# Softmax division of a two-layer graph-attention kernel: all batches on ScalarE, one planner entry per head, and a planner with durations read from a trace

## The chip, the cores and the metric

The kernel runs on one core of one Trainium2 chip. A core has five engines that work side by side and wait for each other through semaphores: TensorE (PE, matmul; its weight loads are shown as PEld), VectorE (DVE), ScalarE (ACT), GpSimd (POOL) and SyncE (SP, which here issues nearly all DMA transfers). The metric is the device time of one execution in microseconds (us). The kernel before takes 2100.86 us, the median of three runs (2097.80 to 2101.08).

## The reference

The input x is 128 batches of a 128 x 512 matrix in fp32, adj is one 128 x 128 adjacency matrix. Layer 0 is a graph step with a maximum, and a layer norm. Layer 1 is masked multi-head attention with a projection, two residual sums and two layer norms:

```python
# layer 0: A = adj @ x[b], C = A + bias
x = layernorm(x + max_over_columns(relu(A[:, None, :] + (C - A)[:, :, None])))
# layer 1: 8 heads of 64 columns
q, k, v = split(x @ w_qkv)
attn = softmax(where(adj == 0, -inf, q @ k.T * 64 ** -0.5))
o = (attn @ v) @ w_proj + b_proj
x = layernorm(x + o + layernorm(o) * gamma + beta)
```

The part that changes is the softmax: of each row of 128 scores in each of 8 heads, the exponentials are divided by their sum.

## The kernel before

**Groups.** The 128 batches are worked in 32 groups of 4. A group is the unit of the main loop (lines 1205 to 1256), and the loop is software-pipelined. One turn p holds, in TensorE's order: the attention product with v of group p-1 (`attend`), the scores of group p (`scores`), v of group p (`v_unit`, seven products instead of eight, with sums of inputs made on GpSimd) with layer 0's matmuls of group p+2 (`l0_mm`) in between, the projection of group p-1 (`o_unit`, also seven products), and q and k of group p+1 (`qk_unit`, 26 products instead of 32; `NODES` and `EDGES` say which product is added to which PSUM bank).

**Names.** k0 to k7 are the eight PSUM banks. u0 to u5 are SBUF copies of banks ("snapshots", ScalarE). s0 to s3 hold the softmax of the four batches of a group. x0 and x1 hold two batches each of layer 0's input, loaded from DRAM in `load`. hl0 to hl8 and so0, so1 are the sums that feed the matmuls. z, xr0 and xr1 belong to the last layer norm (`tails`).

**Softmax, lines 990 to 1076.** For each batch VectorE scales the scores and adds the mask (two instructions on two banks, line 996), then takes the row maximum of all heads (line 1015). ScalarE makes the exponential of each head with its sum (eight instructions, line 1024). VectorE inverts the sums (line 1034). The division follows as eight instructions on 128 x 128 elements: for batches 0 and 2 of a group on ScalarE (`activation` with Identity and a scale column, line 1041), for batches 1 and 3 on VectorE (`tensor_scalar`, line 1043). The table `DIV` (line 988) says which. Then VectorE transposes 32 x 32 blocks into pu (line 1053), SP stores pu to DRAM (hop) and loads it back in four pieces in transposed place into the same s slot, which `attend` of the next turn reads.

**Layer 0 for a later group.** x0 and x1 are read by `l0_mm` and by the layer-norm statistics (`bn`, VectorE, line 430), normalised in place (ScalarE, line 472), transposed in blocks into xt (VectorE, line 507), stored to xhop and loaded back as x1T in four pieces each (SP); then GpSimd adds beta in place and SP spills them to DRAM (`l0_beta_spill`). Only then may SP load the next input into the slot.

**What sets the order.** All work is first recorded with `plan.add(engine, cost, emit, reads, writes)`. Predecessors come from the logs of the buffers. `Plan.run` gives every entry a due time (from the end backwards, with TensorE's entries in a fixed order) and then list-schedules: at each step the engine that can start first takes, of its ready entries, the one due first. Costs, a lag per engine (`LAG`), and for DMAs a shared wire of 270 KB per us (lines 199 and 239 to 241) are its clock. Entries are emitted in that order and each engine keeps it: an engine waits at its next instruction, whatever is ready behind it. One planner entry may be several instructions. Before the change the exponentials and the divisions are entries of four instructions each (lines 1021 to 1047).

**A reuse that the planner does not see.** In `qk_unit` the snapshot of node 1 takes slot u4 (line 751). In the turn's record it comes before `o.closing()`, which is called after node 2 (`between`, line 1252) and whose VectorE result (line 867) still reads the o unit's own snapshot in slot u4 (first the end of `qk_unit`'s loop over the nodes, then the main loop). On the chip the snapshot of node 1 waits for that result.

```python
for fn in between.get(n, ()):
    fn()
...
between = {2: [o.closing]}
```

Of the kernel before, what the change touches and what calls it, by code (L numbers as in the profile page):

```python
# [133 lines left out]
class Op:  # L134
    __slots__ = ("eng", "cost", "lat", "emit", "preds", "succs", "n", "due", "start", "done", "size")

    def __init__(self, n, eng, cost, emit, size):
        self.n, self.eng, self.cost, self.emit, self.size = n, eng, cost, emit, size
        self.preds, self.succs = set(), []
        self.due = self.start = self.done = None  # L140
# [17 lines left out]
class Plan:  # L158
# [5 lines left out]
    def add(self, eng, cost, emit, reads=(), writes=(), size=0):  # L164
        op = Op(len(self.ops), eng, cost, emit, size)
        for accesses, writing in ((reads, False), (writes, True)):
            for a in accesses:
                buf, key = a if type(a) is tuple else (a, None)
                for other, k, w in buf.log:
                    if (w or writing) and (k is None or key is None or k == key):  # L170
                        op.preds.add(other)
                if buf.before is not None and (writing or not buf.log):
                    op.preds.update(o for o, _, _ in buf.before.log)
                buf.log.append((op, key, writing))
        if eng == "PE":
            if self.pe is not None:
                op.preds.add(self.pe)
            self.pe = op
        op.preds.discard(op)
        self.ops.append(op)  # L180
        return op

    LAG = {"PE": 0.27, "DVE": 0.2, "ACT": 0.2, "POOL": 0.15, "SP": 2.2}
    RATE = 0.27

    def run(self, lead):
# [11 lines left out]
        for op in reversed(ops):  # L198
            lag = self.LAG[op.eng] + (op.size / 270.0 if op.size else 0.0)
            due = min((s.due - (0.02 if s.eng == op.eng == "PE" else lag) for s in op.succs), default=end)  # L200
            if op in ideal:
                due = min(due, ideal[op] + op.cost)
            op.due = due - op.cost
        free = dict.fromkeys(self.LAG, 0.0)
        wire = 0.0
# [13 lines left out]
        while todo:  # L219
# [18 lines left out]
            seen = op.done + self.LAG[e]  # L238
            if op.size:
                wire = max(wire, op.done) + op.size / 270.0  # L240
                seen = wire + 2.2
# [12 lines left out]
def kernel(  # L254
# [62 lines left out]
    def dma(dst, src, reads=(), writes=(), kb=512, queue=None, cost=0.47):  # L317
        eng, q = ("ACT", A) if queue == "ACT" else ("SP", SY)
        return plan.add(
            eng, cost, lambda: pin(q.dma_start(out=dst(), in_=src())), reads, writes, size=kb  # L320
        )
# [15 lines left out]
    dma(lambda: adj_sb.t, lambda: adj, [], [adj_sb], 64)  # L337
# [5 lines left out]
    def load(q, queue=None, split=False):  # L343
        b = xs[q] = buf(X_SLOT.get(q, f"x{q % 2}"), [P, 2, D])
        if split:
            for j in range(2):
                dma(lambda j=j: b.t[:, j], lambda j=j: x[2 * q + j], [], [(b, j)], 256, queue)
        else:
            dma(
                lambda: b.t,  # L350
                lambda: x[ds(2 * q, 2)].rearrange("j p d -> p j d"),
                [],
                [(b, 0), (b, 1)],
            )

    load(0, "ACT", True)
    dma(lambda: bias0.t, lambda: l0_b.unsqueeze(1), [], [bias0], 1)
    load(1, None, True)

    def broadcast(name, src, queue=None):  # L360
        b = buf(name, [P, D])
        dma(lambda: b.t, lambda: src.partition_broadcast(P), [], [b], 256, queue)
# [45 lines left out]
    def l0_mm(f, k):  # L408
# [10 lines left out]
        plan.add("DVE", 0.64, lambda: pin(V.tensor_reduce(am.t, b.t, AX.X, ALU.max)), [b], [am])  # L419
# [8 lines left out]
    def bn(src, reads, mv, c):  # L428
        st = small("st", 6)
        plan.add("DVE", 0.64, lambda: pin(V.bn_stats(st.t, src())), reads, [st])  # L430
        plan.add("DVE", 0.17, lambda: pin(V.bn_aggr(mv.t[:, c], st.t)), [st], [(mv, c)])  # L431
# [66 lines left out]
    def l0_transpose(q):  # L498
# [3 lines left out]
        for j in range(2):  # L502
            plan.add(
                "DVE",
                0.64,
# [10 lines left out]
        for i in range(Q):  # L516
# [5 lines left out]
                128,  # L522
            )
        xT = x1T_buf(g)
        for i in range(Q):
# [5 lines left out]
                128,  # L531
# [4 lines left out]
    def l0_transpose_pe(f, k):  # L536
# [5 lines left out]
        def emit():  # L542
# [7 lines left out]
            0.64,  # L550
# [9 lines left out]
    def l0_beta_spill(q):  # L560
# [3 lines left out]
            2.45,  # L564
# [5 lines left out]
        dma(lambda: s.t, lambda: xb.t, [xb], [s])  # L570
# [11 lines left out]
    def weight_forms():  # L582
# [14 lines left out]
        def add(dst, dst_at, a, b, sa, sb_):  # L597
# [3 lines left out]
            if sa < 0 and sb_ < 0:  # L601
                plan.add(
                    "DVE",
                    0.66,
# [9 lines left out]
            if turn % 5 < 3:  # L614
                plan.add("DVE", 0.66, lambda: tt(V, dst(), pa(), pb(), op), reads, [dst_at])
            else:
                plan.add("POOL", 0.74, lambda: tt(GP, dst(), pa(), pb(), op), reads, [dst_at])
# [38 lines left out]
    def qk_plain(h, banks, eng):  # L656

        xT = x1T_buf(0)
        for n in range(4):
# [19 lines left out]
            else:  # L679
                plan.add(  # L680
                    "DVE", 0.64, lambda b=b, n=n: pin(V.tensor_copy(dst.t[:, n], halves(b))), [b], [(dst, n)]
# [4 lines left out]
    def token_sums(g):  # L686
# [6 lines left out]
        for n, (a, b, s) in enumerate(SUMS):  # L693
# [4 lines left out]
                0.74,  # L698
# [15 lines left out]
    def qk_unit(g, phys, between=()):  # L714
# [4 lines left out]
        for n, (prods, lb, chain, seeds, adds, block_) in enumerate(NODES):  # L719
# [14 lines left out]
            if block_ is None:  # L734
                for y, s in mine:
# [3 lines left out]
                        0.66,  # L739
# [16 lines left out]
            else:  # L756
# [3 lines left out]
                for y, s in sorted(mine):  # L760
                    u = snaps[y][0]
                    s = s * SIGN[n]
                    if first:
                        plan.add(
                            "DVE",
                            0.66,
# [12 lines left out]
                    else:  # L779
                        plan.add(  # L780
                            "POOL",
                            1.28,
# [18 lines left out]
    def weight_load(w, src, col):  # L801
        rows = src.rearrange("(d c p) e -> d p c e", d=2, p=P)
        for i, d, c in ((0, 0, 0), (3, 0, HE), (1, 1, 0), (2, 1, HE)):
# [5 lines left out]
                256,  # L809
# [12 lines left out]
    class Unit:  # L822
# [40 lines left out]
        def result(self, half, col):  # L863
# [5 lines left out]
                0.64,  # L869
# [27 lines left out]
    def v_unit(g, phys):  # L897
# [7 lines left out]
        for dst, p, q_, op in (  # L905
# [7 lines left out]
                1.28,  # L913
# [14 lines left out]
    def o_unit(g, phys):  # L928
# [6 lines left out]
        for dst, p, q_, op in (  # L935
# [7 lines left out]
                1.28,  # L943
# [44 lines left out]
    DIV = {0: "ACT", 1: "DVE", 2: "ACT", 3: "DVE"}  # L988

    def softmax(b, bs):  # L990
        s = buf(f"s{b % 4}", [P, 2, NP, P])
        for par in range(2):
            plan.add(
                "DVE",
                0.64,
# [9 lines left out]
                [(s, par)],  # L1005
# [3 lines left out]
        def flat():  # L1009
# [4 lines left out]
            1.17,  # L1014
# [4 lines left out]
        for par in range(2):  # L1019

            def emit(par=par):
                for i in range(4 * par, 4 * par + 4):
                    pin(
                        A.activation(  # L1024
                            flat()[:, i],
                            flat()[:, i],
                            AF.Exp,
                            bias=nm.t[:, i : i + 1],
                            accum_out=sm.t[:, i : i + 1],
                        )  # L1030
                    )

            plan.add("ACT", 1.55, emit, [nm, (s, par)], [(s, par), (sm, par)])
        plan.add("DVE", 0.17, lambda: pin(V.reciprocal(rec.t, sm.t)), [sm], [rec])
        for par in range(2):

            def emit(par=par, eng=DIV[b % 4]):
                for i in range(4 * par, 4 * par + 4):
                    p, r = flat()[:, i], rec.t[:, i : i + 1]
                    if eng == "ACT":  # L1040
                        pin(A.activation(p, p, AF.Identity, scale=r))
                    else:
                        pin(V.tensor_scalar(p, p, r, None, ALU.mult))  # L1043

            plan.add(
                DIV[b % 4], 1.15 if DIV[b % 4] == "ACT" else 0.72, emit, [rec, (s, par)], [(s, par)]
# [4 lines left out]
            1.22,  # L1051
# [14 lines left out]
            [hop],  # L1066
        )
        t = pT[b] = buf(f"s{b % 4}", [P, Q, H, QS])
        for q in range(Q):
# [5 lines left out]
                128,  # L1075
# [30 lines left out]
    def reload(q, slot):  # L1106
        r, s = buf(slot, [P, 2, D]), spilled.pop(q)
        dma(lambda: r.t, lambda: s.t, [s], [r])
        return r

    def tails(g):
# [7 lines left out]
        for h in range(2):  # L1119
# [5 lines left out]
            for j in range(2):  # L1125
# [9 lines left out]
                2.45,  # L1135
# [4 lines left out]
            plan.add("POOL", 2.45, lambda z=z, o=o: tt(GP, z.t, z.t, o.t, ALU.add), [z, o], [z])  # L1140
            plan.add("POOL", 2.45, lambda z=z, r=r: tt(GP, r.t, r.t, z.t, ALU.add), [z, r], [r])
# [140 lines left out]
    dma(wl, lambda: w_proj.rearrange("(c p) e -> p c e", p=P), [], [(lastw, "w")], 1024)  # L1282
# [3 lines left out]
    for q in range(2 * g - 2, 2 * g + 2):  # L1286
# [4 lines left out]
        dma(ap, lambda s=s: s.t, [s], [(lastw, q)], 512)  # L1291
# [8 lines left out]
    def tail_pool(b, o, j):  # L1300
# [6 lines left out]
        for with_, op, rd in (  # L1307
# [5 lines left out]
                "POOL", 1.28, lambda with_=with_, op=op: tt(GP, z(), z(), with_(), op), [zk, rd], [zk]  # L1313
# [3 lines left out]
    def outer(b, zk, z, mz):  # L1317
# [3 lines left out]
        dma(lambda: out[b], z, [zk], [], 256)  # L1321
# [114 lines left out]
```

## Time and profile before

| | |
|---|---|
| median of three runs | 2100.86 us |
| the profiled execution | 2098.84 us |
| its span, first to last instruction | 2097.0 us |
| mean granted TensorE clock | 0.975 |
| busy: PE, PEld | 1932.3 us (92%), 1614.5 us (77%) |
| busy: DVE, ACT, POOL | 1523.7 us (73%), 1339.5 us (64%), 1568.2 us (75%) |
| division on ScalarE, line 1041 | 512 instructions, 159.4 us |
| division on VectorE, line 1043 | 512 instructions, 226.8 us |
| exponentials, line 1024 | 1024 instructions, 395.7 us |
| DMA | 341.87 MB, mean 163 GB/s |

Busy time adds the durations of an engine's instructions; overlapping ones are counted once. In the timeline a row is one instruction or a run of equal ones: start and length in us, engine, source line, operation, output<-inputs with buffer numbers left out, count, and in brackets how long the engine was idle before it and what ended that. Most work that goes through a helper has the helper's line (309, 312, 315, 320), so the tile names tell instructions apart. SPq rows are DMA issues, not transfers. Times inside a turn are given below relative to the first attention matmul of that turn, which is at 1000.54 us in the turn that is used as the example.

### The profile page before, as it was taken

What the parts mean: (1) busy time and instruction counts of PE and PEld (TensorE: products, weight loads), DVE (VectorE), ACT (ScalarE), POOL (GpSimd) and SP (SyncE); (2) the same over time, 40 slices, a digit from 0 to 9 for tenths busy, and PEclk for the clock granted to TensorE, in tenths of its full rate; (3) what the DMA queues carried; (4) which work ended last, traced back from release to release, by engine and by line L of the source; (5) the groups of instructions that cost most, each with busy time, mean ns of one, the idle gap of its engine ahead of it and who ended that gap; (6) DMA issues with size and microseconds to landing.
All of it is one profiled execution on the core that took longest, in us unless ns stands there. A gap on an engine that the chain in (4) does not pass through costs nothing.

```text
span 2097.0 us, 35142 instructions
## 1 busy us (share of the span) xinstructions
PE 1932.3 (92%) x11307; PEld 1614.5 (77%) x11307; DVE 1523.7 (73%) x2906; ACT 1339.5 (64%) x3893; POOL 1568.2 (75%) x1634
## 2 busy tenths in 40 slices
PE   9989899999999989999999999999999999999995
PEld 7777787777787777877778778778777787787883
DVE  8677666777676876767776677766687776777664
ACT  2666565766666666667666667666667665676764
POOL 8657776787776877777777778777777787687856
PEclk9999999999999999999999999999999999999998
DMA  7763466644567445675455764446654456744553
GB/s 220 199 161 106 133 165 201 176 141 147 142 199 201 132 143 149 181 201 169 136 139 161 201 194 137 146 147 181 201 162 142 141 160 201 195 135 131 145 172 128
DMA packets 444855, 341.87 MB, mean 163 GB/s; under 512 B 276736, under 2 KB 378240, under 8 KB 444672
## 3 DMA queue, kind: packets, MB, share of 16 engines
q1 hardware_dynamic: 444384, 339.11, 56.1%
q8 instruction: 90, 1.47, 0.3%
q14 instruction: 93, 0.76, 0.1%
q10 hardware_dynamic: 288, 0.52, 0.1%
HBM read 172.82 MB, written 166.72 MB: 162 GB/s over the span
## 4 chain that ended last, share of the span: by engine, by line
PE 60%; DVE 26%; ACT 5%; DMA 3%; issue 3%; POOL 2%; SPq 1%; ACTq 0%; DVEq 0%; POOLq 0%
PE k L315 60%; DVE s L1043 7%; DVE nm L1015 5%; DVE am L419 3%; DMA x<-in_x_dram 3%; DVE st L430 2%; DVE pu L1053 2%; DVE v L309 2%; SPq L320 1%; ACT s L1024 1%; ACT z L472 1%; DVE qk L312 1%; ACT u L752 1%; POOL x L309 1%; ACT k L748 1%
## 5 line engine op out<-in xcount | busy, mean ns | idle before, releaser
L315 PE MATMUL k<-hl,wqk 128*128 128x256 f32 x2232 | 520.2, 382 | 1.4 <-ACT k L748 1.4
L315 PEld LDWEIGHTS k<-hl,wqk 128*128 128x128 f32 x2232 | 423.6, 191 | 67.7 <-issue 9.4
L1024 ACT ACTIVATE s<-s,nm 128x128 f32<-128x128 f32 x1024 | 395.7, 390 | 3.5 <-DVE nm L1015 3.2
L315 PE MATMUL k<-wv,hl 128*128 128x256 f32 x1024 | 268.8, 410 | 78.9 <-DVE v L309 75.3
L752 ACT COPY u<-k 128x512 f32<-128x512 f32 x341 | 190.1, 589 | 215.6 <-DVE qk L312 142.9
L315 PEld LDWEIGHTS k<-wv,hl 128*128 128x128 f32 x1024 | 204.8, 203 | 146.8 <-DVE v L309 87.3
L315 PE MATMUL k<-x1T,wqk 128*128 128x256 f32 x992 | 252.5, 388 | 58.9 <-ACT u L752 57.8
L309 POOL TENSOR_TENSOR z<-z,ga_bc 128x1024 f32<-128x1024 f32 x60 | 142.0, 2366 | 200.5 <-ACT z L472 200.5
L312 DVE SCALAR_TENSOR_TENSOR qk<-k,u 128x512 f32<-128x512 f32 x248 | 168.4, 687 | 157.4 <-ACT u L752 87.1
L315 PEld LDWEIGHTS k<-x1T,wqk 128*128 128x128 f32 x992 | 187.6, 193 | 99.0 <-ACT u L752 70.3
L315 PE MATMUL k<-wp,so 128*128 128x256 f32 x992 | 241.4, 393 | 0.1
L312 DVE SCALAR_TENSOR_TENSOR s<-k,mask 128x512 f32<-128x512 f32 x256 | 156.4, 682 | 115.3 <-PE k L315 115.1
L309 POOL TENSOR_TENSOR hl<-x1T 128x512 f32<-128x512 f32 (+1 forms) x250 | 216.9, 874 | 28.1 <-PE k L315 16.9
L1043 DVE TENSOR_SCALAR s<-s,rec 128x128 f32<-128x128 f32 x512 | 226.8, 512 | 1.2
L315 PEld LDWEIGHTS k<-wp,so 128*128 128x128 f32 x992 | 199.7, 202 | 32.5 <-DVE o L309 0.8
L309 POOL TENSOR_TENSOR x<-x,be_bc 128x1024 f32<-128x1024 f32 x62 | 146.5, 2362 | 89.4 <-DVE mvo L431 76.7
L309 POOL TENSOR_TENSOR hl<-x1T,hl 128x512 f32<-128x512 f32 (+1 forms) x249 | 196.8, 801 | 0.0
L1024 ACT ACTIVATION_READ_ACCUMULATOR s<-s,nm 128x1 f32 x1024 | 194.1, 190 | 0.0
L315 PE MATMUL k<-wv,x1T 128*128 128x256 f32 x768 | 179.8, 383 | 0.7 <-DVE s L312 0.7
L472 ACT ACTIVATE z<-o,sh,rs 128x512 f32<-128x512 f32 x120 | 97.8, 819 | 124.9 <-POOL xr L309 124.1
L861 ACT COPY u<-k 128x512 f32<-128x512 f32 x189 | 109.1, 577 | 102.0 <-PE k L315 96.4
L315 PE MATMUL k<-wp,oT 128*128 128x256 f32 x744 | 170.7, 379 | 0.0
(142 smaller groups left out, 3592.9 us busy)
## 6 DMA issues: line engine op xcount, KB each, us to landing
hop<-pu SPq DMA_DIRECT2D x128, 512.0 KB, 2.8
s<-hop SPq DMA_DIRECT2D x512, 128.0 KB, 3.3
spill<-x SPq DMA_DIRECT2D x62, 512.0 KB, 4.8
xhop<-xt SPq DMA_DIRECT2D x248, 128.0 KB, 2.6
x1T<-xhop SPq DMA_DIRECT2D x248, 128.0 KB, 4.8
x<-in_x_dram SPq DMA_DIRECT2D x60, 512.0 KB, 5.0
xr<-spill SPq DMA_DIRECT2D x60, 512.0 KB, 5.9
out_dram<-xr SPq DMA_DIRECT2D x60, 512.0 KB, 5.0
```

The source lines that it names most:

```text
L309: pin(eng.tensor_tensor(dst, a, b, op))
L312: pin(V.scalar_tensor_tensor(dst, a, s, b, op0, op1))
L315: pin(PE.matmul(dst, lhsT=lhsT, rhs=rhs, start=start, stop=True, skip_group_check=True))
L419: plan.add("DVE", 0.64, lambda: pin(V.tensor_reduce(am.t, b.t, AX.X, ALU.max)), [b], [am])
L430: plan.add("DVE", 0.64, lambda: pin(V.bn_stats(st.t, src())), reads, [st])
L472: A.activation(dst(), src(), AF.Identity, bias=sh.t[:, i : i + 1], scale=rs.t[:, i : i + 1])
L752: plan.add("ACT", 0.5, lambda b=b, u=u: pin(A.copy(u.t, b.t)), [b], [u])
L861: plan.add("ACT", 0.5, lambda: pin(A.copy(u.t, b.t)), [b], [u])
L1015: lambda: pin(V.tensor_reduce(nm.t, flat(), AX.X, ALU.max, negate=True)),
L1024: A.activation(flat()[:, i], flat()[:, i], AF.Exp, bias=nm.t[:, i : i + 1], accum_out=sm.t[:, i : i + 1],)
L1043: pin(V.tensor_scalar(p, p, r, None, ALU.mult))
L1053: V.transpose(u.t.rearrange("p q h b -> p h q b"), flat().rearrange("p h (q a) -> p h q a", q=Q),)
```

## The change

The division of all four batches of a group is made on ScalarE; `DIV` and the `tensor_scalar` are gone. Every exponential and every division is an entry of its own in the plan, one per head, with one key per head in the buffer log. The planner's costs are changed to other numbers, most of them smaller by 2 to 10%. DMA entries no longer share a modelled wire; each carries a lag of its own (the time from issue to landing), and SP's default lag goes from 2.2 to 5.0 us. The lag between two TensorE entries goes from 0.02 to 0. What TensorE, GpSimd and SP execute is the same set of instructions; VectorE has 512 fewer and ScalarE 512 more. TensorE's order is the same, instruction by instruction. The order on the other four engines is different, and repeats itself over 25 turns.

```diff
-    def add(self, eng, cost, emit, reads=(), writes=(), size=0):
-        op = Op(len(self.ops), eng, cost, emit, size)
+    def add(self, eng, cost, emit, reads=(), writes=(), lag=None):
+        op = Op(len(self.ops), eng, cost, emit, self.LAG[eng] if lag is None else lag)
...
-    LAG = {"PE": 0.27, "DVE": 0.2, "ACT": 0.2, "POOL": 0.15, "SP": 2.2}
-    RATE = 0.27
+    LAG = {"PE": 0.27, "DVE": 0.2, "ACT": 0.2, "POOL": 0.15, "SP": 5.0}
...
-            lag = self.LAG[op.eng] + (op.size / 270.0 if op.size else 0.0)
-            due = min((s.due - (0.02 if s.eng == op.eng == "PE" else lag) for s in op.succs), default=end)
+            due = min(
+                (s.due - (0.0 if s.eng == op.eng == "PE" else op.lag) for s in op.succs), default=end
+            )
...
-            seen = op.done + self.LAG[e]
-            if op.size:
-                wire = max(wire, op.done) + op.size / 270.0
-                seen = wire + 2.2
+            seen = op.done + op.lag
...
-    DIV = {0: "ACT", 1: "DVE", 2: "ACT", 3: "DVE"}
...
-        for par in range(2):
-
-            def emit(par=par):
-                for i in range(4 * par, 4 * par + 4):
-                    pin(
-                        A.activation(
...
-            plan.add("ACT", 1.55, emit, [nm, (s, par)], [(s, par), (sm, par)])
-        plan.add("DVE", 0.17, lambda: pin(V.reciprocal(rec.t, sm.t)), [sm], [rec])
-        for par in range(2):
-
-            def emit(par=par, eng=DIV[b % 4]):
-                for i in range(4 * par, 4 * par + 4):
-                    p, r = flat()[:, i], rec.t[:, i : i + 1]
-                    if eng == "ACT":
-                        pin(A.activation(p, p, AF.Identity, scale=r))
-                    else:
-                        pin(V.tensor_scalar(p, p, r, None, ALU.mult))
-
+        for i in range(H):
+            plan.add(
+                "ACT",
+                0.385,
+                lambda i=i: pin(
+                    A.activation(
...
+                [nm, (s, i)],
+                [(s, i), (sm, i)],
+            )
+        plan.add("DVE", 0.12, lambda: pin(V.reciprocal(rec.t, sm.t)), [sm], [rec])
+        for i in range(H):
             plan.add(
-                DIV[b % 4], 1.15 if DIV[b % 4] == "ACT" else 0.72, emit, [rec, (s, par)], [(s, par)]
+                "ACT",
+                0.295,
+                lambda i=i: pin(
+                    A.activation(
+                        flat()[:, i], flat()[:, i], AF.Identity, scale=rec.t[:, i : i + 1]
+                    )
+                ),
+                [rec, (s, i)],
+                [(s, i)],
             )
```

The lags given to the DMAs are 5.5 us for a load of x0 or x1, 2.7 for hop<-pu, 3.7 for s<-hop, 2.8 for xhop<-xt, 5.5 for x1T<-xhop, 5.8 for spill<-x and 6.3 for xr<-spill.

The orders of one turn that differ and matter below, in the names of the buffers (from the built programs; numbers in brackets count instructions):

```
ACT before, from the last exponentials on:
  exp s3 (8), scale s2 (4), u4 (o unit), scale s2 (4), norm x0, x0, x1, u5 (o unit), k1<-k0, norm x1,
  u4<-k2 (node 1), k3<-k1, norm xr0, u5<-k0, norm xr0, xr1, k4<-k1, k5<-k0, ...
ACT after:
  exp s3 (6), norm x0, u5 (o unit), k1<-k0, scale s3 (1), u4<-k2 (node 1), scale s3 (2), k3<-k1,
  scale s3 (5), norm x0, x1, x1, u5<-k0, norm xr0, k4<-k1, norm xr0, k5<-k0, k6<-k2, norm xr1, xr1, k7<-k4, ...
ACT near the turn's end, before: u4<-k2, norm z, u5<-k1, u0<-k6, norm z, ...
ACT near the turn's end, after:  u4<-k2, u5<-k1, norm z, u0<-k6, norm z, ...
DVE at the turn's start, before: qk, mask+scale s (8), max s0, v, max s1, ... (statistics of x1 later)
DVE at the turn's start, after:  qk, statistics of x0 (2), of x1 (1), mask+scale s (8), max s0, max s1, ...
SP before, from the last pu on: hop, hop, xhop (4), s (4), spill, s (4), x1T (2), out, x1T, xhop (4),
  load x0, spill, x1T, out, xr, x1T (4), load x1, xr
SP after: hop, xhop (4), out, s (4), spill, x1T (2), xhop (4), xr, x1T, spill, x1T, x1T (3), load x0,
  x1T, out, load x1, xr
```

## Prediction

> **What bounds the kernel now.** I read the page's busy times first, then TensorE's waits, then one turn of the main loop in the timeline, engine by engine.
>
> ```profile
> PE 1932.3 (92%) x11307; PEld 1614.5 (77%) x11307; DVE 1523.7 (73%) x2906; ACT 1339.5 (64%) x3893; POOL 1568.2 (75%) x1634
> ```
>
> TensorE is the bound, and its order is not touched. What can be won is its idle time. Its waits:
>
> ```profile
> PE k L315 <- DVE v L309: 75.3, 29, 3.1
> PE k L315 <- ACT u L752: 57.8, 31, 4.3
> ```
>
> Two stalls, each once a turn: 2.66 us for VectorE's v result at 24.9 us into the turn, and 1.72 us for a snapshot near the turn's end. By the starts of the attention matmuls, turns last 62.70 us (809.05 to 871.75) or 64.39 (871.75 to 936.14), on average 64.23 (26 turns, 228.61 to 1898.54). The longer kind loses another 1.7 us to the clock. In windows (length, busy times, then granted clock, DMA share, GB/s):
>
> ```profile
> 1029.50:1033.00 3.50, 3.50 (x10) 2.73 (x10) 2.94 (x9) 1.19 (x4) 2.17 (x4) 0.52 0.62 205
> 1033.00:1065.00 32.00, 30.06 (x138) 25.61 (x137) 19.41 (x41) 19.00 (x34) 19.92 (x22) 1.00 0.95 247
> ```
>
> Right after the first stall the clock is half for 3.5 us. And DMA, quiet on average, is at 0.95 in the second half of a turn. TensorE's own work per turn is 62.70 - 2.66 - 1.72 = 58.3 us.
>
> Why VectorE's v is late is in its timeline, by place in the turn (start at 1000.54):
>
> ```profile
> 1005.38 4.88 DVE L312 SCALAR_TENSOR_TENSOR s<-k,mask 128x512 f32<-128x512 f32 x8 [4.04 <-PE k L315]
> 1019.76 5.22 DVE L1043 TENSOR_SCALAR s<-s,rec 128x128 f32<-128x128 f32 x8
> 1027.43 1.25 DVE L309 TENSOR_TENSOR v<-k,u 128x512 f32<-128x512 f32 x2
> ...
> 1032.33 1.96 DVE L1043 TENSOR_SCALAR s<-s,rec 128x128 f32<-128x128 f32 x8
> ```
>
> The division of batch 1 (5.22 us) and two transposes stand ahead of v. That of batch 3 takes 1.96 us for the same eight instructions.
>
> [...] GpSimd works without a break during the 5.22 us, and mostly has instructions of four columns during the 1.96. ScalarE: [...] the trace has eight in 2.34 us (1019.25 to 1021.59), 292 each. [...]
>
> **The change part by part.** VectorE loses 512 instructions, 226.8 us busy, 7 us a turn. ScalarE gains 512 x 0.292 = 150 us, 4.7 a turn (64% to 71%). Neither sum is the answer; places are. All times below in us from S, the start of VectorE's eight mask instructions (4.84 in the example).
>
> *First stall.* The first exponential starts at S+6.1 (1011.48). Up to snapshot u2 ScalarE now has 17 exponentials x 0.385 (eight take 3.08), 8 divisions x 0.292, 3 copies x 0.5: u2 is done at about S+17.4, v at S+18, 22.8 into the turn; TensorE wants it at 24.9. The stall goes, -2.66, and with it most of the half clock, -1.5 a turn.
>
> *ScalarE then runs without a gap.* Up to seed k1: 32 exponentials 12.3, 24 divisions 7.0, 8 copies 3.9, one norm 0.7: S+30.1, 35.0 into the turn. TensorE wants it at 35.3: hidden, with 0.3 to spare. From here a later S is a stall.
>
> *The snapshot of node 1, and the second stall.* The rows of ScalarE in the kernel before:
>
> ```profile
> 1043.98 0.59 ACT L752 COPY u<-k 128x512 f32<-128x512 f32 x1 [3.06 <-DVE mvo L431]
> 1059.95 0.59 ACT L752 COPY u<-k 128x512 f32<-128x512 f32 x1 [4.47 <-DVE qk L312]
> 1060.43 0.81 ACT L472 ACTIVATE z<-o,sh,rs 128x512 f32<-128x512 f32 x1
> 1061.15 1.06 ACT L752 COPY u<-k 128x512 f32<-128x512 f32 x2
> ```
>
> The first row is the snapshot of node 1 in slot u4: ScalarE idles 3.06 us until VectorE's o result (1043.20 to 1043.89) has read the slot's old content. The wait stays, since neither the slot nor the records changed, but the queue behind it is longer now. The o result needs TensorE's closing product, which follows k1 and one product (S+30.1 + 0.9 + 1.7 = S+32.8), and VectorE, which by then has statistics of its own to finish: done at S+34, between S+33.5 and S+34.5. Behind it ScalarE has the snapshot 0.5, two divisions 0.6 and seed k3 0.5: S+35.6. TensorE, two products of 0.87 after the closing one, wants k3 at S+34.5: a stall of 1.1 (0.2 in some turns before). Then five divisions 1.5, three norms 2.1, u5 0.5, a norm 0.7 and seed k4 0.5: S+40.9. TensorE has only four products (3.5) between k3 and k4: a new stall of 1.8. Before, four such entries, 2.6 us, stood between the two seeds and nothing stalled. Seed k7 costs another 0.1.
>
> The other three rows are the second stall: TensorE waits for the first copy of the last row, and a z norm (0.72 from start to start) stands ahead of it. In the new order the norm comes behind: 1.72 becomes 1.0. TensorE's turn, were nothing else late, is then 58.3 + 1.1 + 1.8 + 0.1 + 1.0 = 62.3.
>
> *The load of x1.* Moved in VectorE's order: the first statistic of x1 now stands ahead of the eight mask instructions; before it came 13 us after S. Behind it in the queue wait the mask instructions, and for them TensorE (their banks take v's products next) and ScalarE's whole block. So x1 has to land before S, and it is the last but one transfer of a long burst on SP's queue:
>
> ```profile
> 1053.65 1.49 SPq L320 DMA_DIRECT2D out_dram<-xr  x1
> 1056.04 6.52 SPq L320 DMA_DIRECT2D x1T<-xhop  x4
> 1062.61 0.66 SPq L320 DMA_DIRECT2D x<-in_x_dram  x1
> ```
>
> By the trace's landings it came at 1067.12, S+61.7[...]. In the new order the burst begins with the store of xr0, whose norm stands behind seed k4 on ScalarE: S+41.6. It lands some 4 us after its issue. Behind it, with the spacing of landings that this burst has (512 KB 1.3, a piece of s 0.55, of x1T 0.6 to 0.8, of xhop 0.37): four s 2.2, spill 1.3, two x1T 1.3, four xhop 1.5, xr 1.5, x1T 0.6, spill 1.3, x1T 0.6, three x1T 2.4, x0 1.3, x1T 0.8, out 1.3, x1 1.3, in all 17.4: S+63. What I can't see is a load that follows stores: x0 after xhop took 3.3 in place of 1.3. None of it and some overlap gives S+62, two of it and a late o result S+66; I take S+64.2. With the statistic (0.7) the next S comes 64.9 after this one. That is a loop from mask to mask through ScalarE, SP and DMA, longer than TensorE's 62.3; the difference of 2.6 is idle TensorE at the banks of the scores and at seed k1.
>
> *Edits at nothing.* GpSimd's order changes by a few places; by its durations its xr sum comes some 3 us earlier, and its sums for q and k keep 2 us or more before TensorE reads them. The transposes pu come up to 7 us later for the last batch, its reload lands by about S+48, 10 us before attention reads it; were that cover gone, each us late would be a us of idle TensorE. The planner's numbers do nothing else than order.
>
> *Sum.* 25 turns x (64.9 - 64.23) = +17; the last turns load nothing and save two or three first stalls, -8. Profiled execution 2098.84 + 9 = 2108; the median of the runs is 2.0 above it: 2110.
>
> **Rivals.** *B, faster:* x1 lands early enough and TensorE's 62.3 decides: 25 x (62.3 - 64.23) - 8 = -56, 2045; with a clock drop in every third turn 2060. For: the landing estimate has 2 us of room, and DMA before the burst is freed of s loads. Against: 0.95 DMA share. It decides where x1 lands before S+61.6. *C, slower still:* the loop holds, and the new stalls of about 2 us halve the clock as 2.66 did: +1.7 a turn, 66.6: 2100.86 + 25 x 2.4 - 8 = 2153. For: waits of 1.7 to 2 us did it in a few turns. Against: most such waits did not. *D, nothing:* ScalarE is as late as VectorE was, and the first stall stays: 2100. Against: 2 us of margin at v.
>
> **How the numbers follow.** A 0.47, with its own range 2085 to 2145 (landing S+63.2 to S+65.6); B 0.33; C 0.17; D 0.03. Forecast 2110. Outside 2045 to 2155 lie about 0.1 of B and 0.1 of C and A. Measurement can tell 0.2%, 4.2 us: below 2096.7 is faster, above 2105.1 slower. Of A some 0.32 is slower, 0.08 same, 0.07 faster; B faster, C slower, D same: faster 0.40, same 0.10, slower 0.50.
>
> **What would show it.** Right: no wait for v at 24.9; waits for k seeds (k3, k4) of 1 to 2 us; VectorE's statistic of x1 ended by the DMA; mask instructions 2 to 3 us later after the attention matmuls; few half-clock windows; turns near 65. Wrong: x1 landed before the scores, turns near 62.3; or no gap at ScalarE's snapshot of node 1, if that wait is gone.

## The result

The changed kernel takes 2108.85 us (median of 11 runs) against 2101.73 us for the kernel before (11 runs): ratio 1.0030, 95% interval 1.0016 to 1.0044. It is slower by 0.3%; the forecast was 2110 us. Its profiled execution has a span of 2101.8 us at a mean granted TensorE clock of 0.981 (before: 2097.0 and 0.975). Line numbers of the changed kernel are four to seven lower than in the kernel before.

The busy times, from the page of the changed kernel:

```profile
PE 1924.2 (92%) x11307; PEld 1608.5 (77%) x11307; DVE 1308.0 (62%) x2394; ACT 1465.9 (70%) x4405; POOL 1561.5 (74%) x1634
```

VectorE has given up 216 us and ScalarE has taken on 126 (the prediction had 226.8 and 150). TensorE is 8 us less busy, and it runs at half clock less: between 200 and 1900 us its granted clock is half for 54.6 us, before for 78.5. What counts is again what TensorE waits for (total us, times, longest):

```profile
PE k L311 <- DVE s L308: 62.1, 26, 4.0
PE k L311 <- ACT u L747: 58.0, 62, 5.5
PE k L311 <- ACT k L743: 25.4, 20, 1.6
...
PE k L311 <- DVE v L305: 0.3, 1, 0.3
```

The first stall (VectorE's v, 75.3 us before) is gone. In its place TensorE waits for the masked scores, a wait that the kernel before did not have, and for ScalarE's seeds (a seed is a copy of one PSUM bank into another, k<-k, to which the next matmuls add). A turn, from attention to attention, lasts 64.48 us on average (26 turns, 227.6 to 1904.1; 64.23 before).

The timeline of VectorE, in the turn that starts at 1647.24, shows where the new wait comes from:

```profile
1654.92 0.69 DVE L425 BATCH_NORM_STATS2 st<-x 128x6 f32<-128x512 f32 x1 [1.64 <-DMA x<-in_x_dram]
1655.53 4.86 DVE L308 SCALAR_TENSOR_TENSOR s<-k,mask 128x512 f32<-128x512 f32 x8
...
1672.56 1.29 DVE L305 TENSOR_TENSOR v<-k,u 128x512 f32<-128x512 f32 x2 [0.54 <-ACT u L856]
```

The statistic of x1 waits for x1's load, and the eight mask instructions stand behind it in VectorE's queue. v comes at 25.3 us into the turn and nobody waits for it. That load stands near the end of a burst on SP's queue (issues near the end of the same turn):

```profile
1693.57 0.40 SPq L315 DMA_DIRECT2D out_dram<-xr  x1
...
1711.11 0.47 SPq L315 DMA_DIRECT2D x<-in_x_dram  x1
```

The burst begins with the store of xr at 1693.57, which is S+38.0 (S is the start of the masks, 1655.53), and x1 is its last transfer but one (the reload of xr follows): it lands at 1717.70, S+62.2. The next masks start at 1718.34. In all 26 turns the masks start 0.63 us after x1's landing. On average the store is issued at S+38.9, x1 lands at S+64.1, and the next masks start at S+64.7. So the loop from mask to mask through the load is real and sets each turn.

The other stall is in ScalarE's timeline of that turn:

```profile
1704.87 1.07 ACT L747 COPY u<-k 128x512 f32<-128x512 f32 x2 [4.47 <-DVE qk L308]
1705.83 0.82 ACT L467 ACTIVATE z<-o,sh,rs 128x512 f32<-128x512 f32 x1
1706.55 0.58 ACT L747 COPY u<-k 128x512 f32<-128x512 f32 x1
1707.01 0.83 ACT L467 ACTIVATE z<-o,sh,rs 128x512 f32<-128x512 f32 x1
1707.73 1.07 ACT L747 COPY u<-k 128x512 f32<-128x512 f32 x2
```

The first copies wait 4.47 us for VectorE's qk result, as before; with no norm between them TensorE's stall is 1.02 us instead of 1.72. But the second z norm now stands ahead of the last two copies, and TensorE waits 0.38 us there.

Node 1's snapshot behaves as predicted in a turn such as the one at 1002.1 (ScalarE, then TensorE):

```profile
1043.92 0.58 ACT L747 COPY u<-k 128x512 f32<-128x512 f32 x1 [3.46 <-DVE o L305]
...
1045.64 1.13 PE L311 MATMUL k<-x1T,wqk 128*128 128x256 f32 x4 [0.80 <-ACT k L743]
```

TensorE stalls 0.80 us at seed k3 and, at 1049.72, 2.08 us at the snapshot after it. Only five of the 26 turns have this (those starting at 227.6, 614.0, 1002.1, 1387.9 and 1773.1), one in six. `snap_buf` rotates through six slots and a turn takes eleven, so node 1 gets slot u4 in every sixth turn only. In the kernel before, the 3.06 us row has the same rhythm.

The half clock has moved with the long stall. In the turn that starts at 680.2 TensorE waits 3.45 us for the masked scores until 691.19 (windows: length, busy times of PE, PEld, DVE, ACT, POOL, then granted clock, DMA share, GB/s):

```profile
691.10:694.60 3.50, 3.41 (x9) 2.80 (x10) 3.50 (x7) 1.52 (x2) 3.50 (x4) 0.57 0.03 12
```

In turns without the half clock TensorE waits 1.6 us more at seed k1 (ScalarE's chain from S). It is the same lateness paid at another place: leaving out the five turns above and two with a half clock of 6.8 us, TensorE stalls at the turn's end 50.46 to 50.62 us after S in the ten turns without the half clock and 50.47 to 50.57 in the nine with it, so in these the half clock itself costs next to nothing.

### The profile page after: what moved, and what is told of

The parts are those of the page before. It is cut to its first block, busy times and chain, and to the rows that moved or that the text cites. A ratio compares the mean times of both kernels' runs of the same rounds, so it can differ in the third digit from the quotient of the medians.

```text
span 2101.8 us, 35162 instructions
## 1 busy us (share of the span) xinstructions
PE 1924.2 (92%) x11307; PEld 1608.5 (77%) x11307; DVE 1308.0 (62%) x2394; ACT 1465.9 (70%) x4405; POOL 1561.5 (74%) x1634
## 4 chain that ended last, share of the span: by engine, by line
PE 46%; ACT 23%; DMA 12%; SPq 7%; DVE 7%; issue 3%; POOL 2%; DVEq 0%; ACTq 0%; POOLq 0%
PE k L311 46%; ACT s L1017 9%; DMA x<-in_x_dram 9%; SPq L315 7%; ACT s L1034 6%; DVE s L308 4%; ACT u L747 2%; DMA s<-hop 2%; ACT u L856 1%; ACT z L467 1%; ACT x L467 1%; POOL x L305 1%; DVE qk L308 1%; ACT k L743 1%; DVE nm L1008 1%
## 5 line engine op out<-in xcount | busy, mean ns | idle before, releaser
L1034 ACT ACTIVATE s<-s,rec 128x128 f32<-128x128 f32 x1024 | 329.0, 394 | 0.9 <-DVE mvo L426 0.9
L747 ACT COPY u<-k 128x512 f32<-128x512 f32 x341 | 186.5, 585 | 186.0 <-DVE qk L308 136.7
L311 PE MATMUL k<-wv,x1T 128*128 128x256 f32 x768 | 203.2, 420 | 62.1 <-DVE s L308 62.1
L311 PE MATMUL k<-wv,hl 128*128 128x256 f32 x1024 | 241.6, 379 | 0.6 <-POOL hl L305 0.6
L1046 DVE STREAM_TRANSPOSE pu<-s 128x1024 f32<-128x1024 f32 x128 | 158.7, 1240 | 132.0 <-ACT s L1034 131.9
L311 PEld LDWEIGHTS k<-wv,hl 128*128 128x128 f32 x1024 | 194.7, 190 | 52.8 <-issue 26.8
L311 PEld LDWEIGHTS k<-wv,x1T 128*128 128x128 f32 x768 | 160.0, 212 | 92.9 <-DVE s L308 67.1
L311 PE MATMUL k<-wp,so 128*128 128x256 f32 x992 | 229.4, 379 | 0.0
L311 PEld LDWEIGHTS k<-wp,so 128*128 128x128 f32 x992 | 188.6, 190 | 25.5 <-issue 0.2
L425 DVE BATCH_NORM_STATS2 st<-x 128x6 f32<-128x512 f32 x128 | 84.2, 678 | 177.5 <-DMA x<-in_x_dram 169.2
```

The costliest lines, as they stand in the source:

```text
L311: pin(PE.matmul(dst, lhsT=lhsT, rhs=rhs, start=start, stop=True, skip_group_check=True))
L425: plan.add("DVE", 0.61, lambda: pin(V.bn_stats(st.t, src())), reads, [st])
L747: plan.add("ACT", 0.5, lambda b=b, u=u: pin(A.copy(u.t, b.t)), [b], [u])
L1034: A.activation(flat()[:, i], flat()[:, i], AF.Identity, scale=rec.t[:, i : i + 1])
L1046: V.transpose(u.t.rearrange("p q h b -> p h q b"), flat().rearrange("p h (q a) -> p h q a", q=Q),)
```

## The experiments

The theory: the load of x1 ahead of the masks makes a loop that sets the turn and takes up what the divisions win. The rivals: ScalarE's longer block sets the turn; or the burst of DMA sets it wherever the statistic stands. Ratios are to the kernel before on the same chip, with 95% intervals.

**x1's statistics behind the masks.** The planner is given one more predecessor; in the steady turns only VectorE's order changes.

```diff
         plan.add("DVE", 0.61, lambda: pin(V.bn_stats(st.t, src())), reads, [st])
+        if behind is not None:
+            plan.ops[-1].preds.add(behind)
...
-            bn(lambda xb=xb, j=j: xb.t[:, j % 2], [(xb, j % 2)], mv, j)
+            bn(lambda xb=xb, j=j: xb.t[:, j % 2], [(xb, j % 2)], mv, j, last_mask if j > 1 else None)
```

> Only VectorE's order changes from the changed kernel: x1's two statistics stand behind the eight mask instructions of their turn, nothing else moves but two places among statistics and transposes. Theory (the mask instructions wait for the load of x1, and this loop sets the 64.5 us of a turn): the wait of TensorE for the masked scores (62.1 us in 26 places) goes, and with it the half clock behind it; a turn is then TensorE's 58.3 + 1.0 + 0.4 + one sixth of 2.9 = 60.2 us, so 2109 - 26 x 4.3 = about 1997, and up to 2045 if the half clock comes back at another place. Rival 1 (ScalarE's longer block sets the turn, and the wait for the masked scores is only where its slack shows): 2100 to 2115, TensorE waiting for ScalarE's seeds and snapshots instead. Rival 2 (the burst of DMA sets the turn wherever x1's statistic stands): between 2050 and 2110, with a wait for x1T or for the reloaded s instead.

Measured: 2040.54 us, ratio 0.9717 (0.9701 to 0.9733). TensorE's wait for masked scores falls from 62.1 to 8.4 us. Two statistics in another place are worth 68 us, so rival 1 falls; but the turn is 62.3, not 60.2. VectorE's timeline says why:

```profile
1041.35 1.29 DVE L426 BATCH_NORM_STATS2 st<-x 128x6 f32<-128x512 f32 x2 [3.96 <-DMA x<-in_x_dram]
...
1042.77 4.86 DVE L308 SCALAR_TENSOR_TENSOR s<-k,mask 128x512 f32<-128x512 f32 x8
```

x0, the last load but one, now holds the masks.

**All four statistics of x behind the masks.**

```diff
-... mv, j, last_mask if j > 1 else None)
+... mv, j, last_mask)
```

> As the run with x1's statistics behind the masks, and x0's two statistics behind them as well; VectorE's order alone changes. Theory: what is left of the wait for masked scores in that run (0.5 to 2 us in most turns) is the load of x0, which lands about 8 us after the turn's start there; without it a turn is 59.9 us, as with the old planner numbers, but for one turn in six with the slot stall (63.3): 1985 to 2000. Rival: the loads are late for the next user too (norms, x1T), and the wait only moves: 2020 to 2040.

Measured: 2027.90 us, ratio 0.9654 (0.9634 to 0.9674). No wait for masked scores is left, but the time is the rival's: the lateness turns up at the next user. Three engines in the turn from 528.1:

```profile
536.77 0.73 POOL L305 TENSOR_TENSOR hl<-x1T 128x256 f32<-128x256 f32 x1 [5.13 <-DMA x1T<-xhop]
...
541.06 1.52 ACT L470 ACTIVATE z<-o,sh,rs 128x512 f32<-128x512 f32 x2 [8.63 <-POOL xr L305]
...
543.10 3.22 PE L311 MATMUL k<-wv,hl 128*128 128x256 f32 x8 [2.16 <-ACT u L859]
```

The first snapshot of v stands behind two z norms, these wait for GpSimd's xr sum, and GpSimd had waited before it for a late x1T. TensorE waits 2.16 us for that snapshot here, and less (0.3 to 1.4 us) in eight other turns. That the late x1T is the cause is read from the trace; it was not tried alone. The larger part of TensorE's waits is for the snapshots in q and k (53.9 us) and for seeds (21.9 us).

**Divisions and entries under the old planner numbers.** The kernel before with the changed `softmax` (divisions on ScalarE, an entry per head, the softmax entries' own new durations). All other durations and the DMA model are the old ones.

```diff
-    DIV = {0: "ACT", 1: "DVE", 2: "ACT", 3: "DVE"}
...
+        for i in range(H):
+            plan.add("ACT", 0.295, lambda i=i: pin(A.activation(
+                flat()[:, i], flat()[:, i], AF.Identity, scale=rec.t[:, i : i + 1])),
+                [rec, (s, i)], [(s, i)])
```

> Half of the change alone: all divisions on ScalarE and one entry per head, while all other durations and the DMA model in the planner are those of the kernel before. In its VectorE order x1's statistics stand behind the mask instructions. Theory (the load of x1 ahead of the masks eats the gain): the first stall of 2.66 us is gone and no new wait for x1 comes; TensorE's turn 60 to 62 us, 1995 to 2050. Rival 1 (ScalarE's longer block sets the turn): 2100 to 2115. Rival 2 (the burst of DMA): 2050 to 2110.

Measured: 1986.48 us, ratio 0.9454 (0.9440 to 0.9468), 8.5 us below the theory's range. The turn is 59.87 us, and 63.3 to 65.0 in one of six. TensorE's longest wait:

```profile
PE k L315 <- ACT u L752: 53.3, 64, 2.1
```

In the loop only the second stall and the slot stall are left. ScalarE's block carries all divisions here and holds nothing up: rival 1 falls for good.

**The planner alone.** The changed kernel with the divisions of batches 1 and 3 on VectorE, one entry per head.

```diff
+            if b % 2 == 0:  # the ScalarE entry as in the changed kernel
...
+            else:
+                plan.add("DVE", 0.18, lambda i=i: pin(V.tensor_scalar(
+                    flat()[:, i], flat()[:, i], rec.t[:, i : i + 1], None, ALU.mult)),
+                    [rec, (s, i)], [(s, i)])
```

> The other half alone: the changed planner (durations, DMA times, one entry per head), but the divisions of batches 1 and 3 on VectorE as before, one entry per head of 0.18 us. In its VectorE order both statistics of x1 stand ahead of the masks. Theory (x1's load holds the masks): TensorE still waits for masked scores, 1 to 3 us a turn, and the stall at VectorE's v may come back: 2095 to 2130. Rival 1 (ScalarE's block): ScalarE is relieved of 4.7 us a turn, the turn falls to about 61, 2010 to 2050.

Measured: 2207.52 us, ratio 1.0504 (1.0489 to 1.0520): slower, as the theory has it, but far outside its range and at another place. In the steady turns the statistics of x stand not only ahead of the masks but ahead of the last qk results. The timeline, three engines, in the turn from 851.5:

```profile
912.05 0.69 DVE L425 BATCH_NORM_STATS2 st<-x 128x6 f32<-128x512 f32 x1 [7.36 <-DMA x<-in_x_dram]
912.66 0.67 DVE L308 SCALAR_TENSOR_TENSOR qk<-k,u 128x512 f32<-128x512 f32 x1
...
913.37 2.05 ACT L747 COPY u<-k 128x512 f32<-128x512 f32 x4 [10.53 <-DVE qk L308]
...
914.49 2.07 PE L311 MATMUL k<-x1T,wqk 128*128 128x256 f32 x4 [7.08 <-ACT u L747]
```

The load holds VectorE, VectorE holds the qk result that frees a snapshot slot, the slot holds ScalarE, and ScalarE holds TensorE, 7.1 us in most turns.

**Entries per head alone.** The kernel before with the same entries and their new durations, the divisions of batches 1 and 3 left on VectorE.

```diff
-            plan.add("ACT", 1.55, emit, [nm, (s, par)], [(s, par), (sm, par)])
+        for i in range(H):  # one exponential each
+            plan.add("ACT", 0.385, ..., [nm, (s, i)], [(s, i), (sm, i)])
...
+            if b % 2 == 0:  # ScalarE, 0.295 each
...
+            else:           # VectorE, tensor_scalar, 0.18 each
```

> The kernel before with one planner entry per head (exponentials and divisions) and nothing else: divisions of batches 1 and 3 stay on VectorE, all other durations and the DMA model are the old ones. The planner puts three of v's results ahead of or between the divisions of batch 1. Theory 1 (the order of VectorE's work made the first stall, and finer entries suffice): the stall at v goes, turn 60 to 61, 1990 to 2030. Theory 2 (VectorE has too much in that stretch, and only moving the divisions helps): the stall at v stays at 1.5 to 2.7, 2065 to 2105.

Measured: 2105.00 us, ratio 1.0015 (1.0003 to 1.0028). TensorE's waits:

```profile
PE k L315 <- ACT u L752: 86.5, 31, 5.1
PE k L315 <- ACT k L748: 33.3, 36, 4.9
PE k L315 <- DVE o L309: 22.0, 27, 0.8
PE k L315 <- DVE v L309: 6.7, 3, 3.1
```

Theory 1 was right about the stall (v: 75.3 to 6.7) and wrong about the time; each expectation holds half of what came. In a typical turn TensorE waits 0.8 us for VectorE's o result, which stands behind the divisions of batch 3 and two transposes, and 0.6 us at seed k1, which stands behind three norms of x on ScalarE. The second stall has grown from 1.72 us to some 3 us, and VectorE's timeline in the turn from 284.7 shows what holds it:

```profile
341.58 0.69 DVE L430 BATCH_NORM_STATS2 st<-x 128x6 f32<-128x512 f32 x1 [3.21 <-DMA x<-in_x_dram]
342.19 0.67 DVE L312 SCALAR_TENSOR_TENSOR qk<-k,u 128x512 f32<-128x512 f32 x1
```

A statistic of x waits for its load ahead of a qk result that ScalarE and TensorE need, here under the old DMA model. Such waits of VectorE add up to 75.9 us in this run, to 29.9 in the kernel before, and to 7.5 in the one with all divisions on ScalarE. So entries alone don't win, but the 118 us between this run and that one are not the divisions' alone: the order of the statistics differs too. What the divisions are worth without the order that comes with them was not tried.

**The new DMA times undone.** The changed kernel with the DMA model of the kernel before (the TensorE lag of 0.02 with it); divisions, entries and durations stay.

```diff
-            seen = op.done + op.lag
+            seen = op.done + self.LAG[e]
+            if op.size:
+                wire = max(wire, op.done) + op.size / 270.0
+                seen = wire + 2.2
```

> The changed kernel with one part undone: the planner's DMA model is the old one (bytes over a shared wire plus 2.2 us, in place of a fixed time for each transfer); ScalarE's divisions, one entry per head and all durations are the changed kernel's. The old model puts x1's and x0's statistics behind the masks and the reload of xr elsewhere on SP's queue. Theory (the new DMA times alone lose what the divisions win): 59.9 us a turn and 63.3 in one of six, 1980 to 2000. Rival (the new durations have a part in it): 2020 to 2109, with TensorE waiting for masked scores or for a snapshot of v.

Measured: 2001.52 us, ratio 0.9520 (0.9503 to 0.9536), 1.5 us above the theory's range. The DMA model (with that lag) costs 107 us of the changed kernel. The new durations cost about 15 (1986.48 to 2001.52): here TensorE waits 0.75 us for masked scores in every other turn. What in the order does that was not followed up.

**Slot u4 for node 1 in every turn.** The changed kernel with the rotation restarted in each turn.

```diff
         banks, snaps = {}, {}
+        u_turn[0] = 3 if 3 < g < 30 else 0
```

> The changed kernel with the rotation of the snapshot slots started anew in each turn, so that node 1's snapshot takes slot u4 in 26 turns and not in one of six. If the reuse of u4 causes the stalls of 0.81 us at seed k3 and 2.08 us at the snapshot bank after it (turns with them average 66.0 us, the others 64.1), they now come in every turn: 21 turns x 1.9 = +40, about 2150; if the wait for x1 takes all of it up, the turns that had a half clock gain something back and it is +20. If the stalls have another cause: 2105 to 2113.

Measured: 2181.04 us, ratio 1.0385 (1.0366 to 1.0403). The slot is the cause, and the price is higher than expected. In the changed kernel the store that begins the burst is issued at S+41.7 in the five slot turns and at S+38.2 in the 21 others, and the masks return after 67.7 and 64.0 us. Now all 26 are of the long kind: 21 x 3.7 = 78, measured 72. The wait lies on the loop.

**Fixed snapshot slots.** The changed kernel with a slot table in place of the rotation: no snapshot takes a slot whose content is still to be read.

```diff
-        u_turn[0] += 1
-        return buf(f"u{slots[u_turn[0] % len(slots)]}", [P, 512])
+        return buf(f"u{SNAP[n]}", [P, 512])
+    SNAP = {1: 0, 3: 3, 8: 1, 9: 2, 10: 4, 11: 5, 14: 3, 17: 4, 18: 2, 20: 5, 21: 1}
```

> The changed kernel with a fixed slot for each of the eleven snapshots in place of the rotation, chosen so that no snapshot takes a slot whose old content is still to be read: no node takes u4 while the o result needs it, and node 14 no longer takes node 1's slot. The order of instructions is the changed kernel's. The waits at seed k3, behind it (0.81 and 2.08, one turn in six) and at the turn's end (1.02 and 0.38, each turn) should all go. Theory (the loop over x1's load sets the turn): TensorE's 1.4 us a turn come back as a longer wait for the masked scores, only the five slot turns gain: 2085 to 2109. Rival (TensorE's own path sets the turn): 26 x 1.4 + 5 x 2.9 = -51, about 2058.

Measured: 2094.15 us, ratio 0.9963 (0.9948 to 0.9979), the theory's case. All snapshot stalls of the loop are gone and come back as a longer wait for the masked scores:

```profile
PE k L311 <- DVE s L308: 116.2, 27, 6.7
```

62.1 us have become 116.2. The 26 turns are no shorter than in the changed kernel (64.57 us on average, and 64.48 there); what is gained lies outside them, most of it ahead of the first. Shortening TensorE's path without the loop gives next to nothing.

**The same table in the kernel before.** The edit is the same.

> The kernel before with the fixed snapshot slots and nothing else. If nothing stands behind TensorE's second stall: it goes (29 x 1.7 = 49), the stall of 2.66 us at VectorE's v stays, with its half clock: about 2050. If a chain through VectorE and the loads is close behind: the stall at v grows or the masked scores are waited for, 2075 to 2101.

Measured: 2033.06 us, ratio 0.9661 (0.9609 to 0.9713). 69 us, more than the 49 of the stall itself (12 us of it are won ahead of the 26 turns, and half clock follows 13 of the 23 waits of 2.66 us, before 19 of 26): turns of 60.71 and about 62.3 us mostly alternate, and the wait for v is the only one left in them:

```profile
PE k L315 <- DVE v L309: 89.9, 29, 6.8
```

The long ones, 6.3 to 6.8 us, come in three turns of about 67 us. In these the eight divisions of batch 1 take 8.7 us on VectorE instead of 5.2; in the one at 236.33 GpSimd works beside them for the first 7.2 us.

**Both causes removed.** The slot table on the kernel with divisions and entries under the old planner numbers, and then on the kernel with the new DMA times undone.

> Division on ScalarE and one entry per head under the old planner numbers (1986 us), with the fixed snapshot slots. If no loop stands behind TensorE's waits: every turn 58.4 to 58.6 us, 1986 - 26 x 1.4 - 5 x 3.4 = 1933. If another chain is close behind (ScalarE's block up to seed k1, the burst of DMA): 1950 to 1986 with new waits for ScalarE's seeds or for x.

> The changed kernel with the old DMA model and the fixed slots together. If the two causes are the whole account of the changed kernel's waits, TensorE waits for nothing in the loop: 57.9 us a turn, 1903 to 1912. If the new durations cost something: above 1915.

Measured: 1908.76 us, ratio 0.9088 (0.9072 to 0.9105), 24 us below the lower expectation, and 1923.85 us, ratio 0.9154 (0.9139 to 0.9169). The first beats both kernels by 9%. Its busy times and longest wait:

```profile
PE 1876.9 (98%) x11307; PEld 1593.5 (84%) x11307; DVE 1312.6 (69%) x2394; ACT 1477.9 (78%) x4405; POOL 1563.2 (82%) x1634
```

```profile
PE k L315 <- DMA s<-hop: 6.4, 2, 4.5
```

In the loop TensorE waits for nothing, each turn lasts 57.92 us, and x1 still lands at S+63.3, after the next masks have begun; what waits for it there costs TensorE nothing. The second kernel is the second of its two cases: the 15 us of the new durations are still there, and with them 14.5 us of waits for masked scores.

## Why the prediction came out right

The sign was right, and so was the mechanism that decided, the loop through the load of x1. That the time came within 1.2 us of 2110 was in part luck. Of the profiled executions (2098.84 and 2103.54 us, 2108 was predicted) the 26 turns grew by 6.6 us together, not by 17, and the rest shrank by 1.8 us, not by 8. The prediction let every turn last as long as a loop. But over the 26 turns S moves from 4.8 to 10.7 us into the turn, so that they are 5.8 us shorter together than 26 loops: loops of 64.7 us make turns of 64.48. The terms one by one:

**First stall.** Right: 75.3 us of waits for v became 0.3. The terms given for snapshot u2 add up to S+16.5 and not to the 17.4 written there; measured it is done at S+17.0. The second half failed, "with it most of the half clock": 12 of 26 turns still have it, before 19. In all twelve the drop comes with a wait for the masked scores, of 2.1 to 4.0 us.

**ScalarE up to seed k1.** The chain was right, S+30.1: in the turn from 1647.24 TensorE goes on at 1685.74, which is S+30.2. The margin of 0.3 held for an early S; with S late it became the predicted stall, 1.6 us. It is the same for every late S, since TensorE too then runs from the masks on.

**Snapshot of node 1.** This step failed. Its wait and its two stalls were sized nearly right in one turn (1.1 and 1.8 predicted, 0.80 and 2.08 measured, the second at the snapshot just ahead of seed k4), and then counted in all turns. The example turn was one of those in which the rotation hands u4 to node 1; the section on the kernel before carries the same reading. Over six turns in succession the same row shows one wait of 3.06 us. The 0.1 us at k7 did not show.

**Second stall.** 1.72 to 1.0 was right (1.02). The 0.38 behind it was not seen: the norm that moved away from the first copies stands ahead of the last ones.

**The load of x1.** The landing was predicted at S+64.2 and the loop at 64.9; measured S+64.1 and 64.7. Two terms were off and cancelled. The burst starts at S+41.6 only where the slot wait delays it, on average at S+38.9. It lasts 25.2 us from that store to x1's landing, not 22.6: in the turn shown three loads of 512 KB land further apart than booked, xr 1.92 us after the piece of xhop ahead of it (1.5 booked), x0 2.42 us after the piece of x1T ahead of it and x1 1.46 us after the store of xr (1.3 each). SP itself waits there too: it stands for 4.68 us after the issue of x1's load and issues the reload of xr at 1716.26, 0.02 us after the store of xr has landed.

**TensorE's turn and rival B.** The 62.3 us contained the slot stalls; without the loop it is 59.9 in five turns of six. So rival B was priced too high: the way to the gain led not to 2045 but to 1986. Rival C, the half clock, was half true: it came at the masks and not at the new stalls, and there the wait at seed k1 makes room for it. Its ground, that waits of 1.7 to 2 us had halved the clock in a few turns before, was misread: of the 26 second stalls before, those of 2.03 and 3.00 us did, and none of the others, which take 1.72 to 1.77.

Put together, taken in this order and against about 2102 us: entries per head alone +3, the divisions on ScalarE with them (and the order that follows) -118, the new durations +15, the new DMA times +107. In another order the steps may be worth something else. The prediction saw the last term as a late load. That it came from the planner's model of DMA times, and that the gain was to be had without it, only the runs showed.

## What to carry to other kernels

A list scheduler that is told a transfer takes a fixed time forgets the queue ahead of it. In the turn shown the load of x1 takes 6.6 us from issue to landing, close to the 5.5 booked, but its issue comes 17.5 us after the store that begins the burst. Instructions that wait for a load are then put ahead of work that others wait for, and the load's lateness becomes everybody's, here 62.1 us of TensorE's waits. (A model with a shared wire is no guarantee: under it too a statistic waited 3.2 us ahead of a qk result, in the run with entries per head alone.) Look for the first instruction on each in-order engine that waits for a DMA, ask what stands behind it, and give it a place by the landing that a trace shows in the loaded queue. When buffers rotate with a count that doesn't divide the turn, read several turns before counting a wait per turn.

## What the hardware showed that was not expected

The same wait came at two prices. In the kernel before with fixed slots TensorE waits for v alone, 2.66 us in 23 of the 26 turns, and the same eight matmuls behind it take 3.45 us in one turn and 1.99 in the next (TensorE's timeline, two turns in succession):

```profile
989.12 1.99 PE L315 MATMUL k<-wv,hl 128*128 128x256 f32 x8 [2.66 <-DVE v L309]
...
1049.85 3.45 PE L315 MATMUL k<-wv,hl 128*128 128x256 f32 x8 [2.66 <-DVE v L309]
```

The granted clock is half after the wait in 13 of 23 such turns, in the kernel before in 19 of 26. What goes with it can be read from the traces. In those of the kernel before and of the changed kernel the 51 and 33 changes of the granted clock all lie on a grid of 3.413 us, to within 3 ns, and between 200 and 1900 us half clock lasts one or two steps of it. The windows below are such steps in the kernel before with fixed slots (length, busy times of PE, PEld, DVE, ACT, POOL, granted clock, DMA share, GB/s):

```profile
984.55:987.97 3.42, 1.92 (x9) 1.33 (x8) 3.42 (x7) 3.28 (x16) 3.40 (x5) 1.00 0.00 0
987.97:991.38 3.41, 2.25 (x10) 2.01 (x11) 3.41 (x9) 3.04 (x16) 0.18 (x1) 1.00 0.77 310
...
1045.99:1049.41 3.42, 1.20 (x6) 0.71 (x4) 3.42 (x7) 3.42 (x18) 2.71 (x4) 1.00 0.14 56
1049.41:1052.82 3.41, 2.97 (x7) 2.44 (x8) 2.49 (x7) 2.62 (x12) 0.00 (x0) 0.50 0.83 305
```

A border of the grid cuts the first wait in two, and TensorE idles 1.50 and 1.16 us in the two steps: the clock stays full. Of the second wait 2.22 us lie in one step, and the next step has half clock. Over the kernel before, the changed kernel and the kernel before with fixed slots, between 200 and 1900 us, all 51 full-clock steps with 2.03 us of TensorE's idle or more (gaps of over 0.1 us between its matmuls) were followed by half clock, 22 of them in the kernel before and 13 in the changed kernel, and none with 2.00 us or less was. These are counts from three traces; what lies behind them is not shown. The alternation fits them: two turns last 122.9 us together, which is 36 steps, so every second turn meets the grid at the same place.
